# Four graph layers in fp32 on one core: the second half of the values moved ahead of the transposes of the exponentials, the adds of x moved behind the sums of k, and two outputs of layer 2's group 2 moved ahead of group 3's mix

## The chip, the cores and the metric

The kernel runs on one core of a Trainium2 chip, in one launch. The metric is the device time of that core in microseconds (us), the median of the runs. All data and all arithmetic are fp32.

## What is computed

The input x holds 128 samples of 64 nodes with 256 features each, 8192 rows ("tokens") in all, and adj is a 64 x 64 matrix that all samples share. Four layers are applied one after the other, each to the normalized and rectified x, and each result is added to x:

```
h = maximum(layernorm(x), 0);  x = x + gnn_lstm(h, adj)       # layer 0
h = maximum(layernorm(x), 0);  x = x + attention(h, W, adj)   # layer 1
h = maximum(layernorm(x), 0);  x = x + gcn(h, adj)            # layer 2
h = maximum(layernorm(x), 0);  x = x + three_slconvs(h, adj)  # layer 3
```

The change is in layers 1 and 2:

```
def attention(h, W, adj):                       # W is 256 x 768, 4 heads of 64
    q, k, v = split(h @ W)                      # per sample and head: 64 x 64 each
    scores = q k^T / 8 + where(adj == 0, -inf, 0)
    return softmax(scores) v                    # 64 x 64 scores per sample and head

def gcn(features, A):                           # W1 256 -> 512, W2 512 -> 256
    agg = A_hat @ features                      # A_hat: normalized A + I, 64 x 64
    h = relu(batchnorm(agg @ W1^T + b1))        # statistics over all 8192 tokens
    return batchnorm(h @ W2^T + b2)
```

Layer 0 is two graph convolutions and LSTMs over windows of one to four nodes. Layer 3 is three products of the form adj * (h W), 256 to 512 to 1024 to 256.

## The kernel before

**Tiles and order.** The 8192 tokens are worked on in 16 groups (`NG`) of 512 tokens (`GN`), that is 8 samples: four tiles of 128 partitions (two samples of 64 nodes) by 256 features. x stays in SBUF as 16 tiles `xs[g]`, and tiles are shared with other data before their x arrives. The code is written in program order; a scheduler in the framework orders the instructions of each engine and sets the semaphores, and `tc.issue_after(i)` keeps what stands inside it behind instruction i in that order. Each engine, and each DMA queue (SyncE's, SP, and GpSimd's, POOL), works through its own list in order. There are 8 PSUM banks of 128 x 512 fp32. One fp32 matmul shows as two records in the trace.

**The attention loop** runs over g = 0 to 15. What iteration g issues, in program order:

- `values(hT_all, v, (0,))`, the first half of the group's values: four matmuls (L1118, 8 records), one ScalarE copy of the bank to `vt` (L1123), and four DMAs on SP's queue (L1126) that put `vt` in order into `v`.
- for g = 4 to 7, `load_x` of x g+8 on SP.
- `queries_keys`: q and k by seven block products instead of eight. Products L1096; copies of two products to `p` on ScalarE (L256); two sums on VectorE (L262, L263). `finish()` adds the rest: the last sum of k on GpSimd (L267, put on the list `sums_on_pool`, whose last entry `summed_last()` gives), a quarter of q on ScalarE (L347), and two more sums on VectorE (L272, L278).
- `add_output(g - 2)`: o = attention output times the reciprocal sum, two VectorE operations (L1204), each followed by one on GpSimd that adds o to x (L1207). Then `sums_of()`, the sums of the exponentials of group g-1 and their reciprocals on VectorE (L1168, L1169).
- `turn(e)`: the exponentials of group g-1 are transposed on TensorE (L1179, 8 transposes, 16 records) into two banks, and each bank is copied by ScalarE to `eT` (L1182).
- `finish()` of the queries and keys.
- only in g = 15: the load of layer 2's first weights, `w1` (L1253), on SP's queue. It goes into the tile that held the weights of q and k, so it waits for the last product that reads them.
- `values(hT_all, v, (1,))`, the second half of the values, as the first. Behind its last DMA: `put_down()`, four DMAs on SP (L396) that write a transposed piece of layer 0's result to DRAM (for groups up to 8).
- `add_turned`: one accumulating DMA on GpSimd's queue (L404) that reads such a piece from DRAM and adds it to an x. It stands behind `shifts_made[g]`, the last GpSimd operation (L997) of the layernorm of group g.
- `features(transposed(h))` for group g+1: h transposed on TensorE (L128, 8 transposes), two ScalarE copies to `hT` (L415), and four differences of blocks of hT on VectorE (L419, L423, L424) for the seven products.
- `attend(eT, v_last)`: exponentials times values of group g-1 (L1192).
- `scores(q, k)`: L1143, and two VectorE operations that scale the scores and add the mask (L1150).
- `softmax`: maximum and subtraction on VectorE (L1161, L1162), the exponential on ScalarE (L1163).
- behind the subtraction: for g < 8 `turn_nodes` (L391, transposes on VectorE of layer 0's result), and `normalized(g + 2)`: the statistics of x (VectorE L991, L993, L994, L996), rstd and nmr on GpSimd (L995, L997), and four ScalarE operations that make h (L112). In g = 14 and 15 the h of layer 2's groups 0 and 1 is made in place of it, also in L112.

So the group whose values are made, the group whose scores are made and the group whose exponentials are turned overlap in one iteration.

**Around the end of the loop**, layer 2 starts: `mixed(g)` multiplies h by the normalized adjacency in 64 x 64 pieces (L146, 64 records) and two copies (L159) evict the two banks; `hidden_products(g, w1, ms)` makes the outputs ms, of four, of the first product (L1022, 4 records each, into one bank each); `hidden_out` takes the statistics of a bank on VectorE (L1033) and copies it to SBUF on ScalarE (L1034).

**Layer 2's loop** runs over g = 1 to 15. For g = 2 on, `mixed(g + 1)` goes ahead of the products of group g; `FREE_FIRST = (2, 3, 0, 1)` is the order of the four outputs. The groups in `SEVEN_FC1` (3, 4, 6, 7, 9, 10, 12) are made by seven block products (`hidden_seven`, L1055), for which `hidden_differences` makes differences of mixed blocks on GpSimd (L1041 to L1043). `rectified(g + 2)` makes h of a later group (L112), `scale(g + 3)` its statistics and scale.

Of the kernel before, what the change touches and what calls it, by code (L numbers as in the profile page):

```python
# [21 lines left out]
NG = NTOK // GN  # L22
# [3 lines left out]
NK = PER  # L26
# [13 lines left out]
def adj_preln_kernel(ctx: ExitStack, tc: tile.TileContext, x_in, adj, vec, bg0, bg1,  # L40
# [9 lines left out]
    def bank(shape=(P, 512)):  # L50
        return psp.tile(list(shape), F32, tag="ps", name="ps")
# [6 lines left out]
    def load_x(x, g):  # L58
        nc.sync.dma_start(out=x, in_=x_view[:, g * GT : (g + 1) * GT, :])
# [63 lines left out]
    def transposed(src):  # L123

        pss = [bank() for _ in range(2)]
        for c in range(2):
            for t in range(GT):
                nc.tensor.transpose(  # L128
                    pss[c][:, t * P : (t + 1) * P], src[:, t, c * P : (c + 1) * P], ident
                )  # L130
        return pss
# [37 lines left out]
    def summed_last():  # L169
        return sums_on_pool[-1]  # L170
# [229 lines left out]
    def add_turned(g):  # L400

        b0 = (g % PER) * GB
        y = ys[g // PER][b0 : b0 + GB].rearrange("(t b) n d -> (b n) t d", b=2)
        nc.gpsimd.dma_start(out=xs[g], in_=y, accum_op=ALU.add)  # L404
# [574 lines left out]
    FREE_FIRST = (2, 3, 0, 1)  # L979
# [33 lines left out]
    def hidden(g, w1, ms=range(4)):  # L1013
        return hidden_out(g, ms, hidden_products(g, w1, ms))

    def hidden_products(g, w1, ms):
        a = h1s[g]
        pss = []
        for m in ms:
            ps = bank()  # L1020
            for c in range(2):
                nc.tensor.matmul(  # L1022
                    ps, lhsT=w1[:, c, m * P : (m + 1) * P], rhs=a[:, 2 + c, :],
                    start=(c == 0), stop=(c == 1),
                )
            pss.append(ps)
        return pss
# [49 lines left out]
    with tc.tile_pool(name="att", bufs=2, reuse_waits="tile") as ap_:  # L1077
        shifts_made, outputs_added = [], []

        def normalized(g):  # L1080
            h = ap_.tile([P, GT, D], F32, tag="h", name="h")
            rstd, nmr, made = ln_on_pool(xs[g])
            ln_apply(xs[g], h, rstd, nmr)
            shifts_made.append(made)
            return h
# [24 lines left out]
        def values(hT, v, ks):  # L1110


            for k in ks:
                ps = bank((P, 2, D))
                for t in range(2):
                    tok = (2 * k + t) * P
                    for c in range(2):
                        nc.tensor.matmul(  # L1118
                            ps[:, t, :], lhsT=hT[:, c, tok : tok + P], rhs=wv[:, c, :],
                            start=(c == 0), stop=(c == 1),  # L1120
                        )
                vt = ap_.tile([P, 2, D], F32, tag="vt", name="vt")
                nc.scalar.copy(vt, ps)  # L1123
                for par in range(2):
                    for b in range(2):
                        last = nc.sync.dma_start(  # L1126
                            out=v[par * 64 : par * 64 + 64, 4 * k + b : 4 * k + 4 : 2, :],
                            in_=vt[b * 64 : b * 64 + 64, :, par * P : (par + 1) * P],
                        )
            return last.ins  # L1130
# [91 lines left out]
        for g in range(NG):  # L1222
            if g == NG - NK + 1:
                turn_pool.__exit__(None, None, None)
                hres_pool.__exit__(None, None, None)
                with tc.using_default_side("right"):
                    ar_right = ctx.enter_context(
                        tc.tile_pool(name="arena_r", bufs=NG // 2, reuse_waits="tile")
                    )
            hT_all, blocks = hT  # L1230
            v = ap_.tile([P, 2 * GT, P], F32, tag="v", name="v")
            moved = values(hT_all, v, (0,))
            if 0 <= g - NK < NK:
                with tc.issue_after(moved):
                    load_x(xs[g + 2 * NK], g + 2 * NK)
            q, k, finish = queries_keys(blocks)
            if g == 0:
                h = normalized(1)
            if last is not None:
                with tc.issue_after(finish.behind):  # L1240
                    if g > 1:
                        add_output(g - 2, pss, ri)
                    sums_of()
            if last is not None:
                e, ri, v_last = last
                if g > 1:
                    eT, turned = turn(e)
            added = finish()
            if g == NG - 1:

                w1 = w_att[:, :, 0:512]
                w2 = w_att[:, :, 512:1024].rearrange("p a (b f) -> a p b f", f=D)
                nc.sync.dma_start(out=w1, in_=w1t.rearrange("(c p) f -> p c f", p=P))  # L1253
            moved = values(hT_all, v, (1,))
            if put_down:
                with tc.issue_after(moved):
                    put_down()
            put_down = None
            if g == 1:

                eT, turned = turn(e)
            if 0 < g <= NG - NK:
                with tc.issue_after(shifts_made[g]):
                    if g > 4:
                        add_turned(g + NK - 1)
            if g + 1 < NG:
                hT = features(transposed(h))
            if g == 0:

                with tc.issue_after(last_copy.ins):  # L1270
                    nc.scalar.activation(rsum, mhalf[:, 0:1], AF.Exp)
            if g == NG - 1:
                turned_in = mixed(0, (on_scalar, on_scalar))
            if last is not None:
                pss = attend(eT, v_last)
            e_next = []

            def masked_scores():
                e, masked = scores(q, k)
                e_next.append(e)  # L1280
                return masked

            if g < NG - 1:
                masked_scores()
            else:
                with tc.issue_after(turned_in), tc.issue_after(added):
                    activated(ar_right, 1, masked_scores)
            ri_next, sub, sums_of = softmax(e_next[0])
            last = (e_next[0], ri_next, v)
            with tc.issue_after(sub):  # L1290
                if g < 8:
                    put_down = turn_nodes(
                        g + 8, tp.tile([P, TN, 2, 32], F32, tag="turned", name="turned")
                    )
                if g + 2 < NG:
                    h = normalized(g + 2)
                elif g + 2 == NG:
                    activated(ar_right, 0)
# [15 lines left out]
        pss = attend(eT, v_last)  # L1314
# [65 lines left out]
    for g in range(1, NG):  # L1380
        if g == 1:
            mixed(2, (on_scalar, on_scalar))
            counted[1] += hidden(1, w1, range(2))
        else:
            if g + 1 < NG:
                seven_next = g + 1 in SEVEN_FC1
                mixed(g + 1, (on_scalar, on_scalar if seven_next else on_vector))
                if seven_next:
                    hidden_differences(g + 1, fc1_t(g + 1))
            if g == SEVEN_FC1[-1] + 1:  # L1390
                for a in range(2):
                    nc.sync.dma_start(
                        out=w2[a], in_=w2t.rearrange("(a b p) f -> a p b f", a=2, p=P)[a]
                    )
            if g in SEVEN_FC1:
                counted.append(
                    hidden_seven(
                        g, fc1_w, fc1_t(g), lambda: rectified(g + 2), lambda last: scale(g + 3, last)
                    )
                )  # L1400
                continue
            pss = hidden_products(g, w1, FREE_FIRST)
            counted.append(hidden_out(g, FREE_FIRST[:1], pss))
            with tc.issue_after(evicted[-1]):
                last = rectified(g + 2)
            with tc.issue_after(last) if last else nullcontext():
                counted[g] += hidden_out(g, FREE_FIRST[1:], pss[1:])
        scale(g + 3, counted[g][2 if g == 1 else 0].ins)
        if g == 1:
            with tc.issue_after(evicted[-2]):  # L1410
                rectified(3)
# [92 lines left out]
    for g in range(NG):  # L1504
# [20 lines left out]
        else:  # L1525
            pss = first_pss[g] if g < 2 else [bank() for _ in range(2)]
# [369 lines left out]
    for g in range(NG + 1):  # L1896
# [13 lines left out]
        if s3 is not None:  # L1910
            pss = [bank((P, 2, D)) for _ in range(2)]
            if g == NG:
                pss = [pss, [bank((P, 2, D)) for _ in range(2)]]
# [92 lines left out]
```

## Time and profile before

| | us |
|---|---|
| three runs | 2420.54, 2420.59, 2421.62 |
| median | 2420.59 |
| the profiled execution, its own time | 2423.3 |
| its span in the trace | 2421.5 |

The busy time of each engine in stretches of the trace. The attention loop takes the third stretch, layer 2's first products are in the fourth.

| stretch, us | TensorE | VectorE | ScalarE | GpSimd | granted clock | DMA share |
|---|---|---|---|---|---|---|
| 0 to 600 (layer 0) | 595.30 | 463.77 | 350.23 | 172.43 | 1.00 | 0.08 |
| 600 to 1190 (layer 0) | 589.26 | 393.92 | 270.04 | 110.68 | 1.00 | 0.13 |
| 1190 to 1417 (layer 1) | 222.13 | 195.46 | 126.28 | 84.27 | 1.00 | 0.47 |
| 1417 to 1700 (layer 2) | 279.08 | 200.52 | 166.62 | 95.16 | 0.99 | 0.07 |
| 1700 to 2421 (layer 3) | 712.91 | 431.77 | 264.08 | 143.39 | 1.00 | 0.12 |

Times in the trace count from the start of the span. A line of the timeline gives the start, the duration, the engine, the line of the kernel, the operation, what is written and read, the shapes, the count of records that were merged, and in brackets how long the engine was idle before it and which engine and line ended that idle time. PE is a matmul on TensorE, PEld the load of its stationary operand, DVE is VectorE, ACT is ScalarE, POOL is GpSimd, SP is SyncE, and "q" behind an engine's name is its own queue of issues. A line of a table by stretches gives the stretch, its length, the busy time (and number of records) of PE, PEld, DVE, ACT and POOL, the granted TensorE clock (1.00 is full speed), the DMA share and GB/s.

### The profile page before, as it was taken

The numbers are of one execution on the slowest core, as the hardware profiler recorded it, in microseconds if no ns is written. First come the engines' busy times: TensorE is split into PE (matmuls) and PEld (weight loads), VectorE is DVE, ScalarE is ACT, GpSimd is POOL, SyncE is SP. The second block draws the span as 40 slices with busy tenths as digits, with TensorE's granted clock in tenths as the row PEclk, the third lists the DMA queues.
The fourth block names the chain that finished last, engine by engine and source line by source line (L and its number), as shares of the span: only waits on it lengthen the run. The fifth ranks groups of instructions, "written<-read, shape, count | busy, mean of one in ns | idle before, by whom it ended". The sixth has DMA issues, their size and how long they took to land.

```text
span 2421.5 us, 49124 instructions
## 1 busy us (share of the span) xinstructions
PE 2398.7 (99%) x20272; PEld 2094.3 (86%) x20272; DVE 1685.4 (70%) x3425; ACT 1177.2 (49%) x2178; POOL 605.9 (25%) x549
## 2 busy tenths in 40 slices
PE   9999999999999999999999999999999999999999
PEld 7778888889999999988888867586898999999998
DVE  6768888777566687775599887586556655665664
ACT  4557755555444454453455556564333334333332
POOL 4432222222111112212224444123111311221121
PEclk9999999999999999999999999999999999999999
DMA  4200000001000000053347410010133100000000
GB/s 139 86 2 1 1 18 1 1 1 35 1 1 1 1 1 1 18 127 70 53 78 133 76 32 2 10 62 10 27 62 57 33 10 11 19 10 10 19 10 19
DMA packets 163712, 75.45 MB, mean 31 GB/s; under 512 B 104481, under 2 KB 159905, under 8 KB 163489
## 3 DMA queue, kind: packets, MB, share of 16 engines
q1 hardware_dynamic: 150096, 59.18, 9.8%
q0 software_dynamic: 12672, 12.58, 3.5%
q8 instruction: 159, 2.61, 0.4%
q14 instruction: 65, 0.52, 0.1%
q10 hardware_dynamic: 720, 0.56, 0.1%
HBM read 42.94 MB, written 20.97 MB: 26 GB/s over the span
## 4 chain that ended last, share of the span: by engine, by line
PE 92%; DVE 5%; ACT 2%; issue 1%; POOL 0%; DVEq 0%; ACTq 0%; POOLq 0%
PE ps L704 37%; PE ps L1772 13%; PE ps L1824 8%; PE ps L197 7%; PE ps L1700 4%; PE ps L146 4%; PE ps L1096 3%; PE ps L612 2%; PE ps L638 2%; PE ps L1470 2%; PE ps L1022 2%; PE ps L1055 2%; PE ps L1532 1%; PE ps L1118 1%; PE ps L1845 1%
## 5 line engine op out<-in xcount | busy, mean ns | idle before, releaser
L718 ACT ACTIVATE gates<-gates,lbias 128x512 f32<-128x512 f32 (+3 forms) x482 | 265.7, 605 | 173.7 <-DVE gates L272 121.6
L704 PE MATMUL ps<-diff,s 128*128 128x256 f32 (+1 forms) x1600 | 344.9, 369 | 0.5 <-DVE diff L826 0.5
L704 PEld LDWEIGHTS ps<-diff,s 128*128 128x128 f32 x1600 | 303.3, 190 | 27.5 <-issue 0.9
L1772 PE MATMUL ps<-arena 128*128 128x256 f32 x1408 | 318.5, 380 | 0.0
L267 POOL TENSOR_TENSOR gates<-p 128x512 f32<-128x512 f32 (+1 forms) x115 | 148.9, 1295 | 589.0 <-DVE p L263 518.4
L1772 PEld LDWEIGHTS ps<-arena 128*128 128x128 f32 x1408 | 261.4, 190 | 35.1 <-issue 2.0
L704 PE MATMUL ps<-h,w 128*128 128x256 f32 (+1 forms) x1028 | 242.5, 371 | 0.0
L704 PE MATMUL ps<-diff,w 128*128 128x256 f32 (+1 forms) x1040 | 239.7, 371 | 0.0
L704 PEld LDWEIGHTS ps<-diff,w 128*128 128x128 f32 x1040 | 194.8, 190 | 16.5
L704 PEld LDWEIGHTS ps<-h,w 128*128 128x128 f32 x1028 | 192.7, 190 | 17.7 <-issue 0.5
L267 POOL TENSOR_TENSOR arena<-arena 128x512 f32<-128x512 f32 (+1 forms) x80 | 91.7, 1147 | 461.9 <-DVE arena L263 407.8
L256 ACT COPY p<-ps 128x512 f32<-128x512 f32 (+1 forms) x262 | 142.1, 563 | 60.1 <-PE ps L704 39.7
L350 ACT ACTIVATE arena<-arena 128x512 f32<-128x512 f32 x168 | 98.5, 624 | 121.4 <-POOL arena L267 66.5
L256 ACT COPY arena<-ps 128x512 f32<-128x512 f32 (+1 forms) x160 | 82.2, 517 | 149.6 <-PE ps L1700 59.5
L1824 PE MATMUL ps<-arena 128*128 128x128 f32 x1280 | 149.1, 275 | 0.8 <-DVE arena L339 0.8
L1824 PEld LDWEIGHTS ps<-arena 128*128 128x128 f32 x1280 | 146.7, 192 | 2.1 <-DVE arena L339 1.2
L718 ACT ACTIVATE gates<-ps,lbias 128x256 f32<-128x256 f32 (+2 forms) x157 | 68.2, 479 | 143.9 <-PE ps L704 143.8
L339 DVE TENSOR_TENSOR arena<-arena 128x512 f32<-128x512 f32 (+1 forms) x192 | 111.3, 612 | 29.4 <-ACT arena L350 27.8
L207 ACT COPY free<-ps 128x128 f32<-128x128 f32 x104 | 27.6, 265 | 208.0 <-PE ps L197 208.0
L272 DVE TENSOR_TENSOR gates<-p,ps 128x512 f32<-128x512 f32 (+1 forms) x115 | 76.3, 664 | 65.0 <-PE ps L704 64.2
L704 PE MATMUL ps<-state,s 128*128 128x256 f32 (+1 forms) x512 | 116.3, 370 | 0.6 <-ACT p L256 0.6
L272 DVE TENSOR_TENSOR arena<-arena,ps 128x512 f32<-128x512 f32 (+1 forms) x80 | 48.1, 601 | 87.0 <-PE ps L1824 50.4
(270 smaller groups left out, 4831.0 us busy)
## 6 DMA issues: line engine op xcount, KB each, us to landing
x<-in_x SPq DMA_DIRECT2D x23, 512.0 KB, 4.0
y<-turned SPq DMA_DIRECT2D x64, 128.0 KB, 3.3
v<-vt SPq DMA_DIRECT2D x128, 64.0 KB, 2.6
w<-in_wih SPq DMA_DIRECT2D x4, 1024.0 KB, 7.2
x_for_h<-in_x SPq DMA_DIRECT2D x8, 512.0 KB, 6.9
x<-y POOLq DMA_DIRECT2D x8, 512.0 KB, 6.3
x_for_h<-y POOLq DMA_DIRECT2D x8, 512.0 KB, 6.7
z<-w SPq DMA_DIRECT2D x64, 64.0 KB, 2.0
```

What stands on the lines that cost most here:

```text
L146: last = nc.tensor.matmul(pss[b][half * 64 : half * 64 + 64, c, t, :], lhsT=src[rows, t, col : col + 64], rhs=a2[rows, :], start=True, sto ...
L197: nc.tensor.matmul(q[k], lhsT=w, rhs=b, start=first and k == 0, stop=True, skip_group_check=True)
L256: copied = nc.scalar.copy(p1 if i == 1 else p5, ps[i])
L267: nc.gpsimd.tensor_tensor(out=out[1][1], in0=p1, in1=p5, op=ALU.add).ins
L272: nc.vector.tensor_tensor(out[0][1], p1, ps[5], ALU.add)
L339: last = eng.tensor_tensor(out=s, in0=p, in1=q, op=op)
L350: nc.scalar.activation(o, o, func)
L704: nc.tensor.matmul(ps[:, r], lhsT=wc[:, j, :], rhs=bc, start=first and r == 0 and c == 0, stop=True, skip_group_check=True,)
L718: nc.scalar.activation(o, ps, func, bias=lbias[:, col : col + 1])
L1700: nc.tensor.matmul(ps[:, t, :], lhsT=w[:, t * P : (t + 1) * P], rhs=b, start=first and t == 0, stop=True, skip_group_check=True,)
L1772: nc.tensor.matmul(ps[:, r, :], lhsT=w[:, c, col : col + P], rhs=b[:, c, :], start=first and r == 0 and c == 0, stop=c == 1, skip_group_ch ...
L1824: nc.tensor.matmul(ps[:, t, :], lhsT=w[:, c, t * P : (t + 1) * P], rhs=b[:, c, :], start=first and t == 0 and c == 0, stop=c == 3, skip_gr ...
```

## The change

Three edits of order; no operation is added or removed, apart from the number of the group to which an add of x belongs.

1. In the attention loop `values(hT_all, v, (1,))` now stands ahead of `turn(e)`, of `finish()` and, in g = 15, of the load of `w1`. It stood behind these three.
2. `add_turned` stands behind `summed_last()`, the last sum of k on GpSimd, where it stood behind the layernorm of group g. It runs for g = 4 to 11 and takes x g+4, where it ran for g = 5 to 12 and took x g+3. Both make the adds for x 8 to 15, the changed kernel one iteration earlier.
3. In layer 2's loop, g = 2: the outputs 2 and 3 of group 2 (`FREE_FIRST[:2]`) are issued ahead of `mixed(3)`, and the outputs 0 and 1 behind it. All four were behind it.

```diff
@@ attention loop, g = 0 to 15
                     sums_of()
+            moved = values(hT_all, v, (1,))
             if last is not None:
                 e, ri, v_last = last
                 if g > 1:
                     eT, turned = turn(e)
             added = finish()
             if g == NG - 1:
                 w1 = w_att[:, :, 0:512]
                 w2 = w_att[:, :, 512:1024].rearrange("p a (b f) -> a p b f", f=D)
                 nc.sync.dma_start(out=w1, in_=w1t.rearrange("(c p) f -> p c f", p=P))
-            moved = values(hT_all, v, (1,))
             if put_down:
                 with tc.issue_after(moved):
                     put_down()
@@
-            if 0 < g <= NG - NK:
-                with tc.issue_after(shifts_made[g]):
-                    if g > 4:
-                        add_turned(g + NK - 1)
+            if NK <= g < NG - NK:
+                with tc.issue_after(summed_last()):
+                    add_turned(g + NK)
@@ layer 2, g = 2 to 15
+            pss = hidden_products(g, w1, FREE_FIRST[:2]) if g == 2 else []
             if g + 1 < NG:
                 seven_next = g + 1 in SEVEN_FC1
                 mixed(g + 1, (on_scalar, on_scalar if seven_next else on_vector))
@@
-            pss = hidden_products(g, w1, FREE_FIRST)
+            pss += hidden_products(g, w1, FREE_FIRST[len(pss) :])
```

`NK` is 4, so `NG - NK` is 12.

## The prediction

> **What bounds the kernel now.** I read the page first, then the timeline of the attention groups engine by engine, then the timeline and the granted clock at the start of layer 2.
>
> ```profile
> span 2421.5 us, 49124 instructions
> PE 2398.7 (99%) x20272; PEld 2094.3 (86%) x20272; DVE 1685.4 (70%) x3425; ACT 1177.2 (49%) x2178; POOL 605.9 (25%) x549
> PE 92%; DVE 5%; ACT 2%; issue 1%; POOL 0%; DVEq 0%; ACTq 0%; POOLq 0%
> ```
>
> By the page TensorE is the bound. Stage by stage that is not so. One attention group (group 3), from one maximum L1161 to the next:
>
> ```profile
> 1239.81 1.22 DVE L1161 TENSOR_REDUCE mx<-e 128x16 f32<-128x1024 f32 x1
> ...
> 1243.57 0.86 PEld L1179 LDWEIGHTS ps<-ident,e 128*128 128x128 f32 x8 [0.31 <-ACT e L1163]
> ...
> 1247.20 2.08 ACT L112 ACTIVATE h<-x_for_h,nmr,rstd 128x256 f32<-128x256 f32 x4 [0.97 <-POOL nmr L997]
> ...
> 1249.18 0.57 ACT L1123 COPY vt<-ps 128x512 f32<-128x512 f32 x1
> ...
> 1249.69 1.08 ACT L415 COPY hT<-ps 128x512 f32<-128x512 f32 x2
> ...
> 1250.80 0.69 DVE L419 TENSOR_TENSOR hT<-hT 128x512 f32<-128x512 f32 x1 [0.79 <-ACT hT L415]
> ...
> 1252.33 1.28 DVE L1150 SCALAR_TENSOR_TENSOR e<-ps,mask 128x512 f32<-128x512 f32 x2
> ...
> 1253.65 1.22 DVE L1161 TENSOR_REDUCE mx<-e 128x16 f32<-128x1024 f32 x1
> ```
>
> The reader is to see a closed loop of 13.84 us: VectorE works without a gap from L1161 to the statistics, GpSimd makes nmr, ScalarE starts h 7.39 after L1161, hT's copies start 2.49 after h, L419 1.11 after them, L1150 1.53 after L419, the next L1161 1.32 later. Each waits for the one before. TensorE's own work in a group is less: group 14 ran in 13.59, start to start, with hardly a wait. So ScalarE's place in this loop is worth time, and TensorE's small waits are not.
>
> In groups 6 to 8 the loop is 15.10, 15.39 and 15.08, since GpSimd's k meets L419:
>
> ```profile
> 1291.97 1.72 POOL L267 TENSOR_TENSOR k<-p 128x512 f32<-128x512 f32 x1
> 1292.32 1.93 DVE L419 TENSOR_TENSOR hT<-hT 128x512 f32<-128x512 f32 x1 [0.81 <-ACT hT L415]
> ```
>
> L419, else 0.69, ends 0.56 after GpSimd does (1293.69, 1294.25).
>
> **The change, part by part.**
>
> *Values ahead of the transposes.* TensorE does the same matmuls: eight records of L1118 (1.73 us) now run in front of L1179. They cover the waits for the exponentials (0.31 above in the loader, 0.07 to 0.54 in the matmuls). I cost this at nothing, because the loop does not pass through L1179; were the loop gone, it would be worth the sum over groups 9 to 14, some 1.7, and about 1.3 in groups 2 to 8. But the built program's order moves ScalarE too. In groups 2 to 8 between h and hT stood one copy (vt, L1123); now stand the second eT copy (L1182) and q (L347), because vt goes ahead of h. One operation more, at the step of such copies, 0.48 (in group 9: 1335.08, 1335.54, 1336.02, 1336.51). So each of groups 2 to 5 takes 0.48 more: +1.92. In groups 9 to 14 the order becomes h, vt, eT, eT, q, hT: four operations. The trace has that count in group 9:
>
> ```profile
> 1333.10 2.08 ACT L112 ACTIVATE h<-x_for_h,nmr,rstd 128x256 f32<-128x256 f32 x4 [1.32 <-POOL nmr L997]
> ...
> 1336.97 1.09 ACT L415 COPY hT<-ps 128x512 f32<-128x512 f32 x2
> ```
>
> 3.87 from h to hT, and a loop of 14.06 (without the transposes L391 h starts 6.21 after L1161: 6.21 + 3.87 + 1.13 + 1.52 + 1.32). Groups 9 to 14 took 14.06, 13.80, 13.91, 14.01, 13.55 and 13.60; at 14.06 each the change is 0, +0.26, +0.15, +0.05, +0.51, +0.46: +1.43. Groups 0 and 1 keep their path.
>
> *Adds of x behind the sums of k.* By the built order GpSimd does k first, then the add's issue (L404), then the two L1207; the adds also start a group earlier, so group 8 has none. In groups 6 and 7 k is no longer late, but L1207 takes its place: k ends 1.19 after h starts, L404 takes 1.3, two L1207 2.54: GpSimd is busy until 5.03 after h, L419 is ready at 2.97 + 1.11 = 4.08 and would end at 4.77, and so ends at 5.59. The loop is 14.32 + 0.82 = 15.14, against 15.10 and 15.39: +0.04 and -0.25. Group 8 is 14.32 against 15.08: -0.76. No row shows L1207 holding up L419 for long; I price it by k's row, as the same operation on the same shapes. Bounds: no hold (-0.82 for each of two groups, -1.6), or a hold by the whole 1.24 of the row above (+0.8). Sum of both parts over groups 2 to 14: 1.92 + 1.43 + 0.04 - 0.25 - 0.76 = +2.4.
> [...]
>
> *The load of layer 2's weights.* This is what the diff hides. In group 15 values now stands ahead of the load of w1 (L1253) in the program and on SP's queue, where a transfer that waits holds up those behind it.
>
> ```profile
> 1417.18 0.40 SPq L1253 DMA_DIRECT2D w<-in_w1t  x1
> 1419.45 0.57 ACT L1123 COPY vt<-ps 128x512 f32<-128x512 f32 x1
> 1420.05 3.37 SPq L1126 DMA_DIRECT2D v<-vt  x4
> 1421.82 3.70 PE L1022 MATMUL ps<-arena,w 128*128 128x512 f32 x8
> ```
>
> Now w1 is issued as soon as the last product has read the old weights, 1417.18, and its landing takes 3.4 (the row of this transfer): 1420.6, 1.2 ahead of L1022. After the change it stands behind four v transfers that wait for vt, and ScalarE does vt right after the four L112 (h starts 7.18 after L1161, here too). vt ends 2.55 after h, four issues take 2.5 to 3.4 (such rows: 2.54, 2.61, 2.93, 3.37), the landing 3.4: w1 is there some 9.2 after h. L1022 started 4.83 after h (1416.99): +4.4. No other TensorE work stands in between, since its queue is in order. Bounds: 2.5 for the issues and the 2.6 that a v transfer takes to land, +3.3; 3.4 and the 5.1 of a 1024 KB load, +6.1. Without this reordering the cost is 0, and I see no gain in it. The old slack of 1.2 is used up within these figures.
>
> *Two outputs of group 2 ahead of group 3's mix.* There TensorE waits for L112 and then runs slow:
>
> ```profile
> 1441.58 1.44 PE L146 MATMUL ps<-ah,arena 64*64 64x64 f32 x48 [1.37 <-ACT arena L112]
> 1443.50:1444.50 1.00, 1.00 (x6) 0.07 (x5) 0.40 (x1) 0.00 (x0) 0.92 (x2) 0.51 0.00 0
> ```
>
> The granted clock is 0.5 from 1443.5 to about 1446.9: 3.4 us at half speed, 1.7 lost. Before: from the end of group 1's outputs (1440.06) to the end of group 3's products (1459.52) 19.4. After, by rows: wait for L159 0.2, eight records of L1022 3.55, mix L146 1.05, eight records 3.55, mix 1.05. ScalarE now does group 4's L112 (ready at 1446.0 by nmr, 2.08) and an eviction before it copies group 3's mix: the copies end about 1449.6, GpSimd's L1041 at 1450.9. So a wait of 0.2, one product 0.86, a wait of 0.55, six products 5.3. Together 16.3: -3.1. With no wait at all it would be -3.9; if the late copies cost twice as much, -2.3.
>
> *Clock after the new stall.* TensorE idles some 4.3 us before L1022. No row shows so long a wait; the nearest is the 1.37 above, followed by 3.4 us at half clock: +1.7. Bounds: 0, and two such stretches less the idle part, +2.7. I take +1.7.
> [...]
>
> **Sum:** +2.4 + 4.4 + 1.7 - 3.1 = +5.4. The profiled execution took 2423.3 (span 2421.5 and 1.8 around it), 2.7 over the median of the runs, 2420.59; the difference is put on the median: 2426.0, +0.22%. With each term at its end: -1.6 - 1.1 - 1.7 - 0.8 below and +0.8 + 1.7 + 1.0 + 0.8 above; not all at once, so the forecast's own range is 2422.5 to 2429.5.
>
> **Rivals.**
> 1. *w1 comes in time* (SP's transfers pass each other, or vt is done earlier). For it: only one load; against it: the built order and the 1.2 of slack. The terms 4.4 and 1.7 fall away: 2419.9.
> 2. *ScalarE's order costs nothing and the loop opens.* TensorE then sets the pace in attention: the covered exponentials (3.0) and k's three waits of 0.58 (1.7) come off, and w1 is hidden; with layer 2's 3.1: 2412.8, faster. For it: TensorE is 99% busy and the waits named at L1179 and L1143 are the ones edited. Against it: periods of 13.84, 13.83 and 13.83 with VectorE idle for one wait of 0.79. It decides if h comes no later and hT's copies follow it by 2.49 or less.
> 3. *The clock falls in attention too.* The loop leaves TensorE idle 0.5 to 1.5 per group, split up; in group 15 about 1.3 around L146. Half clock twice more: +3.4, 2429.4. Against it: groups 6 to 8 had such idle time at full clock.
>
> **How the numbers follow.** Forecast 0.57, rival 1 0.15, rival 2 0.13, rival 3 0.15. The likeliest gives 2426.0. The range runs from 2418.5 (below rival 1) to 2430.5 (above rival 3) and leaves out rival 2 and a little above: 2 in 10. A difference of 0.2% (4.8 us) is about what a measurement can tell from none: over 2425.4 lie a good half of the forecast and rival 3, 0.48; under 2415.8 rival 2, 0.12; the rest, 0.40, between.
>
> **What would show it.** Groups 2 to 5 at 14.3 from L1161 to L1161, with L1182 and L347 between L112 and L415; groups 9 to 14 at 14.06; no wait left at L1179; L419 stretched in groups 6 and 7 by L1207 and not in 8; w1's load behind four v loads and L1022 waiting some 4 us for it; half clock after that and none at group 3's mix. I am wrong if those groups run at 13.6, or if L1022 follows the scores at once.

## The result, and the profile after

The changed kernel took 2431.47 us (median of 6 runs, 2428.85 to 2432.59) against 2421.56 for the kernel before on the same chip (6 runs, 2420.54 to 2424.14): a ratio of 1.0038, interval 1.0026 to 1.0051. It is slower by about 9.9 us. The forecast had the side right and the amount too small: 2426.0, and 2431.47 lies above the end of its range, 2430.5.

The first lines of the page of the changed kernel, its busy times and the shares of the chain that ended last:

```profile
span 2430.8 us, 49154 instructions
PE 2399.5 (99%) x20272; PEld 2099.4 (86%) x20272; DVE 1681.9 (69%) x3425; ACT 1174.7 (48%) x2178; POOL 606.2 (25%) x549
PE 91%; DVE 5%; ACT 2%; issue 1%; POOL 1%; DMA 1%; SPq 0%; DVEq 0%; ACTq 0%; POOLq 0%
```

The work is the same (20272 records on TensorE in both), and TensorE's busy time has hardly moved (2398.7 before). Of the 9.3 us between the two spans 0.8 are busy time of TensorE; the rest is waiting. New in the chain is a DMA, 1%. The page can't say more, since a share is a mean over all stages.

Group 3 of the attention loop in the timeline of the changed kernel (start, duration, engine, line; all engines, the lines of the loop picked out):

```profile
1242.25 1.22 DVE L1161 TENSOR_REDUCE mx<-e 128x16 f32<-128x1024 f32 x1
...
1249.63 2.08 ACT L112 ACTIVATE h<-x_for_h,nmr,rstd 128x256 f32<-128x256 f32 x4 [1.08 <-POOL nmr L997]
...
1251.62 0.56 ACT L1182 COPY eT<-ps 128x512 f32<-128x512 f32 x1
...
1252.09 0.58 ACT L347 ACTIVATE q<-ps 128x512 f32<-128x512 f32 x1
...
1252.57 1.05 ACT L415 COPY hT<-ps 128x512 f32<-128x512 f32 x2
...
1253.65 0.69 DVE L419 TENSOR_TENSOR hT<-hT 128x512 f32<-128x512 f32 x1 [1.21 <-ACT hT L415]
...
1256.50 1.22 DVE L1161 TENSOR_REDUCE mx<-e 128x16 f32<-128x1024 f32 x1
```

Two ScalarE operations, eT and q, now stand between h and hT, where vt alone stood before. hT starts 2.94 after h (2.49 before), L419 waits 1.21 for it (0.79 before), and the group takes 14.25 (13.84 before).

The end of the loop, TensorE alone, then the granted clock in stretches (start and end, length, busy time and records of PE, PEld, DVE, ACT, POOL, then the clock, 0.50 in the second row):

```profile
1425.03 1.14 PE L1143 MATMUL ps<-k,q 64*64 64x64 f32 x63
1430.64 5.37 PE L1022 MATMUL ps<-arena,w 128*128 128x512 f32 x8 [4.48 <-DMA w<-in_w1t]
1435.94 1.16 PE L146 MATMUL ps<-ah,arena 64*64 64x64 f32 x64
```

```profile
1430.00:1431.00 1.00, 0.36 (x1) 0.30 (x2) 0.16 (x1) 0.81 (x1) 0.00 (x0) 1.00 0.01 2
1431.10:1434.50 3.40, 3.40 (x5) 1.35 (x4) 0.52 (x1) 0.15 (x1) 0.00 (x0) 0.50 0.00 0
1435.00:1439.00 4.00, 4.00 (x72) 2.22 (x71) 2.95 (x12) 1.91 (x4) 0.02 (x1) 1.00 0.01 4
```

TensorE waits 4.48 for w1, and then runs 3.4 us at half clock: eight records of L1022 take 5.37, where they took 3.70.

All profiles of this case side by side, cut at the same instructions. "Values" is the first L1118, the next columns run from there to the first L1022, from that to the first L1055, to the first L1700 (layer 3), to the end of the last matmul, and to the end of the span. The last column counts TensorE's waits for its own instructions ("issue") in front of L146 in layer 3, and their sum. The kernels other than the two are those of the experiments below.

| kernel | start to values | to L1022 | to L1055 | to L1700 | layer 3 | rest | waits at L146 |
|---|---|---|---|---|---|---|---|
| before | 1197.27 | 224.55 | 31.46 | 211.67 | 752.53 | 4.03 | 4, 3.7 |
| before_again | 1199.35 | 224.59 | 29.89 | 211.67 | 752.57 | 4.01 | 4, 3.5 |
| after | 1199.29 | 231.35 | 29.23 | 211.66 | 753.94 | 5.34 | 6, 4.9 |
| after_again | 1199.03 | 231.53 | 29.19 | 211.66 | 754.73 | 4.01 | 6, 5.3 |
| w1_first | 1199.29 | 226.46 | 27.91 | 211.98 | 755.66 | 4.71 | 7, 6.1 |
| l2_only | 1197.25 | 224.63 | 27.90 | 211.98 | 752.22 | 4.01 | 4, 3.0 |
| values_only | 1196.48 | 227.71 | 31.46 | 211.67 | 755.29 | 5.92 | 7, 5.6 |
| adds_only | 1197.29 | 223.91 | 29.89 | 211.68 | 753.13 | 4.01 | 4, 4.1 |
| adds_last | 1196.21 | 220.73 | 27.90 | 211.97 | 752.57 | 4.02 | 4, 3.5 |
| values_middle | 1197.25 | 224.07 | 27.82 | 211.97 | 754.03 | 4.01 | 4, 4.0 |
| pad64 | 1201.22 | 225.39 | 29.89 | 211.66 | 756.62 | 4.01 | 7, 7.2 |

So between the two first profiles 2.0 come before the change begins, 6.8 from attention with the load of w1, -2.2 from layer 2, +1.4 from layer 3, and +1.3 from the last landing. Only the second and third belong to lines that the change touches. Whether the others belong to it was the first question.

### The profile page after: what moved, and what is told of

It is laid out like the page before. It is cut to its first block, busy times and chain, and to the rows that moved or that the text cites. A ratio compares the mean times of both kernels' runs of the same rounds, so it can differ in the third digit from the quotient of the medians.

```text
span 2430.8 us, 49154 instructions
## 1 busy us (share of the span) xinstructions
PE 2399.5 (99%) x20272; PEld 2099.4 (86%) x20272; DVE 1681.9 (69%) x3425; ACT 1174.7 (48%) x2178; POOL 606.2 (25%) x549
## 4 chain that ended last, share of the span: by engine, by line
PE 91%; DVE 5%; ACT 2%; issue 1%; POOL 1%; DMA 1%; SPq 0%; DVEq 0%; ACTq 0%; POOLq 0%
PE ps L704 37%; PE ps L1772 13%; PE ps L1824 8%; PE ps L197 7%; PE ps L1700 4%; PE ps L146 4%; PE ps L1022 3%; PE ps L612 3%; PE ps L638 2%; PE ps L1470 2%; PE ps L1055 2%; PE ps L1096 2%; PE ps L1532 1%; PE ps L1118 1%; ACT h L112 1%
## 5 line engine op out<-in xcount | busy, mean ns | idle before, releaser
L1772 PE MATMUL ps<-arena 128*128 128x256 f32 x1408 | 318.4, 381 | 0.0
L1772 PEld LDWEIGHTS ps<-arena 128*128 128x128 f32 x1408 | 262.0, 191 | 34.4 <-issue 1.7
```

The costliest lines, as they stand in the source:

```text
L1772: nc.tensor.matmul(ps[:, r, :], lhsT=w[:, c, col : col + P], rhs=b[:, c, :], start=first and r == 0 and c == 0, stop=c == 1, skip_group_ch ...
```

## The experiments

### The kernel before and the changed kernel once more

> The kernel before, unchanged. Theory (some of the difference is not of the change): the stretch up to the first values, 1197.3 us in the first profile, and the landing of the last output differ from run to run by up to 2 us, while layer 3 has the same four waits of TensorE for its own instructions at the same matmuls as before (0.86, 1.09, 1.19, 0.60, sum 3.7), since they come from the place of the instructions in the program. Rival (these waits are chance as well): other waits, at other matmuls. Time 2420.5 to 2424.

> The changed kernel, unchanged. Theory: from the first values to layer 3 it takes 4.6 more than the kernel before (472.3 against 467.7), and layer 3 has the same six waits for instructions as in its first profile (sum 4.9, 1.1 more than before): 2421.6 + 5.7 = 2427.3, and what is above that is the start-up (1199.3 instead of 1197.3 up to the first values) and the last landing, by chance. Rival (the start-up is slower by the change): again 1199 or more up to the first values, 2431.

before_again: 2423.92 us against 2421.93 for the runs beside it, ratio 1.0003 (0.9994 to 1.0012). after_again: 2430.71, ratio 1.0034 (1.0021 to 1.0046).

The stretch up to the values was 1197.27 and 1199.35 for the same kernel: that difference is chance (what it goes with is in the last section). Layer 3 repeats: four waits at L146 in both profiles of the kernel before, at the same instructions, six in both of the changed one. So the 1.4 to 2.2 of layer 3 belong to the change, though no line of layer 3 is in it. The forecast of 2427.3 for the changed kernel was too low again.

before_again had a surprise in layer 2. TensorE alone, at group 3's mix, and the granted clock behind it:

```profile
1443.71 1.44 PE L146 MATMUL ps<-ah,arena 64*64 64x64 f32 x48 [1.38 <-ACT arena L112]
1445.08 1.13 PE L1022 MATMUL ps<-arena,w 128*128 128x512 f32 x2
1446.14 0.46 PE L146 MATMUL ps<-ah,arena 64*64 64x64 f32 x16
1446.53 6.28 PE L1022 MATMUL ps<-arena,w 128*128 128x512 f32 x14
```

```profile
1445.50:1448.90 3.40, 3.40 (x24) 1.50 (x23) 1.73 (x4) 1.60 (x4) 3.11 (x5) 1.00 0.02 5
```

The same wait, 1.38, but the clock stays at 1.00, and the stretch to L1055 takes 29.89, not 31.46. Of the five profiles without the edit in layer 2, two fell to half clock here (31.46) and three did not (29.89). More executions agree: of 73 of the kernel before, 23 have a mean granted clock of 0.998 or 0.999 and 50 of 1.000 (one stretch of 3.4 us at half clock takes 0.0007 off the mean). So at most about a third of them fell here.

### The load of w1

In the changed kernel, group 15 alone makes the second half of its values behind the load:

```diff
-            moved = values(hT_all, v, (1,))
+            if g < NG - 1:
+                moved = values(hT_all, v, (1,))
...
                 nc.sync.dma_start(out=w1, in_=w1t.rearrange("(c p) f -> p c f", p=P))
+                moved = values(hT_all, v, (1,))
```

> The changed kernel, but group 15 makes the second half of its values behind the load of layer 2's weights, as before the change. Theory: the load is issued when the last product has read the old weights, the 4.45 of waiting in front of L1022 and the half clock behind it (1.67) go, from the first values to L1022 it takes 224.55 + 2.1 = 226.7 (231.35 in the changed kernel), and the time falls by 6.1 to 6.5, to some 2425. Rival (another wait takes the place of the load, such as the copies of eT or the scores): 229 or more to L1022, and 2429 or more.

2425.23 us, ratio to the kernel before 1.0014 (1.0005 to 1.0022), so 5.5 to 6.2 less than the changed kernel. SP's queue and L1022 in the timeline of the changed kernel, and then of w1_first:

```profile
1413.77 12.96 SPq L1126 DMA_DIRECT2D v<-vt  x8
...
1422.88 0.56 ACT L1123 COPY vt<-ps 128x512 f32<-128x512 f32 x1
...
1426.83 0.54 SPq L1254 DMA_DIRECT2D w<-in_w1t  x1
```

```profile
1421.07 0.40 SPq L1255 DMA_DIRECT2D w<-in_w1t  x1
1423.96 3.48 SPq L1126 DMA_DIRECT2D v<-vt  x4
...
1425.74 3.70 PE L1022 MATMUL ps<-arena,w 128*128 128x512 f32 x8
```

In the changed kernel the load stands behind eight v transfers, of which the last four wait for the vt of 1422.88; it is issued at 1426.83 and L1022 starts 3.8 later. In w1_first it is issued at 1421.07 and waits for nobody's vt: L1022 comes with no wait, at full clock (3.70). From the values to L1022 it takes 226.46 (expected 226.7). By the stretches of the table this is the largest single cost of the change: 231.35 against 226.46 up to L1022, and 29.23 against 27.91 behind it.

### Layer 2's edit alone

```diff
+            pss = hidden_products(g, w1, FREE_FIRST[:2]) if g == 2 else []
...
-            pss = hidden_products(g, w1, FREE_FIRST)
+            pss += hidden_products(g, w1, FREE_FIRST[len(pss) :])
```

> The kernel before with the edit in layer 2 alone. Theory: no wait for L112 and no half clock at group 3's mix; from the first L1022 to the first L1055 27.6 instead of 31.5 (less 1.37 of waiting, 1.7 of clock and the rest of the mix in pieces), 2421.6 - 3.9 = 2417.7; layer 3's waits for instructions as before (one instruction of TensorE more). Rival (only the wait goes, the clock falls elsewhere): 29.3 and 2419.4. Rival (the late copies of group 3's mix take it back): 31 and 2421.

2419.55 us, ratio 0.9991 (0.9982 to 1.0001): a gain of 2.4, at the edge of what can be told. To L1055 it took 27.90, near the 27.6 of the theory; but the theory counted from 31.46, and 29.89 is as common. Layer 2 after it is 0.3 longer (211.98). So the edit brings 1.7 where the clock would have held and 3.25 where not. Four kernels have this edit and get w1 in time. In three of them (l2_only, and adds_last and values_middle below) the mean granted clock is 1.000 in all 31 runs; w1_first has 3 of 11 below that, and in the profiled one of these the half clock is at the start.

### Values alone, adds alone

values_only is the kernel before with this alone, so that group 15 keeps its order:

```diff
                     sums_of()
+            if g < NG - 1:
+                moved = values(hT_all, v, (1,))
...
                 nc.sync.dma_start(out=w1, in_=w1t.rearrange("(c p) f -> p c f", p=P))
-            moved = values(hT_all, v, (1,))
+                moved = values(hT_all, v, (1,))
```

adds_only is the kernel before with this alone:

```diff
-            if 0 < g <= NG - NK:
-                with tc.issue_after(shifts_made[g]):
-                    if g > 4:
-                        add_turned(g + NK - 1)
+            if NK <= g < NG - NK:
+                with tc.issue_after(summed_last()):
+                    add_turned(g + NK)
```

> The kernel before with the values moved alone, and group 15's behind the load of w1. Theory (ScalarE's place in the loop): groups 2 to 5 at 14.25 and 9 to 14 at 14.05 from one maximum to the next, as in the changed kernel; 6 to 8 15.1 to 15.5, since k still meets L419; from the first values to L1022 224.6 + 3.1 = 227.7 or a little more. TensorE has 33 instructions more, so layer 3 has six or more waits for instructions at its mixes (before: four). Rival (the adds make the groups longer, not ScalarE): 13.83 in groups 2 to 5 and 224.6 or less.

> The kernel before with the adds of x moved alone. Theory: groups 2 to 5 at 13.83; in groups 6 and 7 k comes in time and L1207 holds L419 by 0.8, 14.7; group 8 13.84; one of groups 9 to 11, where one L1207 stands between L995 and L997 on GpSimd, up to 1.2 longer; from the first values to L1022 222.7 to 224 (224.6 before). [...] Rival (the adds make the loop longer): 14.2 in groups 2 to 5. TensorE's instructions are as many as before: four waits in layer 3's mixes.

From one maximum to the next (the difference of the starts of L1161), in us:

| groups | before | after | values_only | adds_only | adds_last | values_middle |
|---|---|---|---|---|---|---|
| 2 | 13.77 | 14.19 | 14.19 | 13.78 | 13.76 | 14.19 |
| 3, 4, 5 (mean) | 13.83 | 14.25 | 14.26 | 13.84 | 13.83 | 14.26 |
| 6 | 15.10 | 15.10 | 15.10 | 15.10 | 13.85 | 14.27 |
| 7 | 15.39 | 15.08 | 15.39 | 15.10 | 13.87 | 14.29 |
| 8 | 15.08 | 14.26 | 15.10 | 13.85 | 13.86 | 14.28 |
| 9 to 14 (mean) | 13.82 | 14.05 | 14.06 | 13.97 | 13.85 | 13.91 |

values_only: 2430.30 us, ratio 1.0031 (1.0019 to 1.0043), and 227.71 to L1022, as expected. The values alone, with w1 in time, are the slower loop. Of the 7.6 us between the medians that is 3.2; in the profile layer 3 is 2.7 longer and the last landing 1.9 longer than in the kernel before. adds_only: 2421.19, ratio 0.9997 (0.9988 to 1.0006). Group 8 came as expected, 6 and 7 not: 15.10, not 14.7. The timeline of group 6 in adds_only says why:

```profile
1288.69 1.26 POOL L267 TENSOR_TENSOR k<-p 128x512 f32<-128x512 f32 x1
...
1289.91 1.30 POOL L404 DMA_DIRECT2D x_for_h<-y  x1
...
1290.75 3.00 POOL L1207 TENSOR_TENSOR x_for_h<-x_for_h,o 128x512 f32<-128x512 f32 x2
1292.37 1.94 DVE L419 TENSOR_TENSOR hT<-hT 128x512 f32<-128x512 f32 x1 [0.81 <-ACT hT L415]
```

L419 starts 0.4 earlier behind h than in the changed kernel (3.60 against 4.03) but does not end before L1207: it ends at 1294.31, 0.56 after GpSimd (1293.75), the same 0.56 as behind k in the kernel before. The group's end is set by when GpSimd is done, so the hold simply takes up what L419 was earlier.

### The adds behind GpSimd's other work

If so, the add's issue (L404, 1.3) must not stand ahead of L1207. adds_last is the kernel before with the edit in layer 2 and

```diff
+            if NK <= g < NG - NK:
+                with tc.issue_after(summed_last()), tc.issue_after(outputs_added[-1]):
+                    add_turned(g + NK)
```

in place of the add of the kernel before. One more line differs, in adds_last and in values_middle: the sums of blocks of layer 2's weights on GpSimd (`sums(nc.gpsimd, *fc1_a[0], *fc1_a[1], *fc1_s)`) stand behind `summed_last()` too, and not behind `outputs_added[-1]` alone. No run has that line by itself; behind L1022 adds_last and l2_only take the same time up to layer 3 (27.90 and 211.97 or 211.98).

> The kernel before with the edit in layer 2, and the adds of x behind the sums of k and behind both L1207 of the group as well; values and load of w1 as before. Theory: with GpSimd's order k, L1207, L1207, L404 neither k nor L1207 meets L419; groups 6 to 8 at 13.84 instead of 15.10, 15.39 and 15.08 (less 4.0), one of groups 9 to 11 up to 1.2 longer; with layer 2's 2.0, 2421.9 - 4.8 to - 6.0 = 2416 to 2417. Rival (L1207 still holds L419): 14.7 in groups 6 and 7, 2418.

2416.15 us, ratio to the kernel before 0.9977 (0.9967 to 0.9986): faster than both, by the adds and the edit in layer 2 together. Group 6 in its timeline:

```profile
1287.57 1.27 POOL L267 TENSOR_TENSOR k<-p 128x512 f32<-128x512 f32 x1
...
1288.80 2.53 POOL L1207 TENSOR_TENSOR x_for_h<-x_for_h,o 128x512 f32<-128x512 f32 x2
1291.24 1.30 POOL L404 DMA_DIRECT2D x_for_h<-y  x1
1291.24 0.69 DVE L419 TENSOR_TENSOR hT<-hT 128x512 f32<-128x512 f32 x1 [0.80 <-ACT hT L415]
```

Now L1207 is done as L419 starts, and L419 takes 0.69. The issue L404 beside it holds nothing up. Groups 6 to 8 are at 13.85 to 13.87, and attention to L1022 is 220.73, 3.8 less than before.

### TensorE's order or ScalarE's?

values_only moves two things: TensorE makes the values ahead of the transposes, and ScalarE's copies change places. values_middle is adds_last with this:

```diff
                     eT, turned = turn(e)
+            if g < NG - 1:
+                moved = values(hT_all, v, (1,))
             added = finish()
...
                 nc.sync.dma_start(out=w1, in_=w1t.rearrange("(c p) f -> p c f", p=P))
-            moved = values(hT_all, v, (1,))
+                moved = values(hT_all, v, (1,))
```

TensorE's transposes then go ahead of these values, as before; but between h and hT ScalarE does vt and q.

> The kernel adds_last with the second half of the values between the transposes of the exponentials and the rest of the products (group 15 as before, behind the load of w1). TensorE then makes the transposes ahead of these values, as in the kernel before; on ScalarE vt and q stand between h and hT, two operations, as eT and q do in the changed kernel (one in the kernel before). Theory (the count of copies between h and hT sets the group): groups 2 to 5 at 14.25, 6 to 8 at 14.25 or a little more, from the first values to L1022 2.5 to 4 longer than in adds_last (220.73). Rival (TensorE's order, values ahead of transposes, made the groups longer): 13.84 and 220.7.

2419.36 us, ratio 0.9987 (0.9977 to 0.9996), a smaller gain than that of adds_last. Groups 2 to 8 at 14.19 to 14.29, and to L1022 224.07, 3.3 more than in adds_last. ScalarE in group 3:

```profile
1247.59 2.08 ACT L112 ACTIVATE h<-x_for_h,nmr,rstd 128x256 f32<-128x256 f32 x4 [1.99 <-POOL nmr L997]
1249.58 0.57 ACT L1123 COPY vt<-ps 128x512 f32<-128x512 f32 x1
1250.04 0.59 ACT L347 ACTIVATE q<-ps 128x512 f32<-128x512 f32 x1
1250.53 1.06 ACT L415 COPY hT<-ps 128x512 f32<-128x512 f32 x2
```

Two operations between h and hT, vt and q where the changed kernel has eT and q, and the same 2.94 from h to hT; the groups take 14.26. Values ahead of the transposes are not the cause, since here they stand behind them. ScalarE's rows have no gap from h to hT, and L419 waits for hT: the count of operations there is what makes the group longer.

### Sixteen small products at the start

Why does layer 3 change? Its waits of TensorE are for "issue", for nothing that another engine does. Counting TensorE's records in the trace in order of their start, from 0 (weight loads, matmuls and waits on semaphores), the waits of 0.6 and more in front of L146 stand at numbers 30657, 31681, 35521 and 36545 before, and 28865, 30657, 31681, 32705, 36545 and 37569 after: all 193 more than a multiple of 256. The page of the kernel before lists among the DMA queues (queue, kind: packets, MB, share of 16 engines):

```profile
q8 instruction: 159, 2.61, 0.4%
```

Each packet of it in the trace has 16384 bytes (16 KB), and the trace has 160 of them, the last one behind the span. TensorE's program has 40897 records there, which in pieces of 256 are 160 as well. From these two counts, a packet for each 256 instructions of TensorE is an estimate of the author's. The waits go with the packets: in all eleven profiles each of the 57 waits in front of L146 ended 1.2 to 1.6 us after a packet of this queue did. So they are taken here as waits for instructions. The changed order gives TensorE 36 instructions more (386 waits on semaphores in place of 350), so everything behind stands elsewhere in its pieces of 256. To test this, the kernel before was given 64 instructions more:

```diff
             keep_busy(7)
+            for i in range(16):
+                half = slice(i % 2 * 64, i % 2 * 64 + 64)
+                nc.tensor.matmul(
+                    idle[half, 0:1], lhsT=ones[half, 0:64], rhs=ones[half, 0:1],
+                    start=True, stop=True,
+                )
```

> The kernel before with 16 small products (64 x 64 by one column, 64 instructions of TensorE) more at the start, while TensorE waits for adj; nothing of them is used. Theory (layer 3's waits come where the 16 KB pieces of TensorE's instructions end inside a mix): all instructions behind move by 64 places, and layer 3's mixes have eight or nine waits instead of four, at other matmuls, layer 3 takes 756 to 758 instead of 752.5, though nothing of it was changed. Rival (chance, or transfers at the same time): the same four waits at the same matmuls, 752.5.

2429.59 us, ratio 1.0028 (1.0016 to 1.0040). Some 3 of it are the start (the products delay the first values to 1201.22) and 0.8 is attention; layer 3 took 756.62, as expected, with seven waits at L146 (eight or nine were expected). One spot, TensorE in the kernel before and then in pad64, which is here 4.5 us later:

```profile
1913.43 0.61 PE L1845 MATMUL ps<-arena,w2s 64*64 64x256 f32 x8
1913.86 0.51 PE L146 MATMUL ps<-w2s,arena 64*64 64x64 f32 x20
1915.23 0.92 PE L146 MATMUL ps<-w2s,arena 64*64 64x64 f32 x44 [0.86 <-issue]
```

```profile
1917.96 0.61 PE L1851 MATMUL ps<-arena,w2s 64*64 64x256 f32 x8
1918.40 1.11 PE L146 MATMUL ps<-w2s,arena 64*64 64x64 f32 x64
1919.44 5.45 PE L1778 MATMUL ps<-arena 128*128 128x256 f32 x24
```

The wait there is gone, and others have come, at 1825.72, 2013.61 and 2061.39 among them, where the kernel before has none. In all eleven profiles such waits stand 193 or 194 past a multiple of 256, and where one kernel was profiled twice they are at the same matmuls. So in these runs the waits go by the place of the instructions, and each ends 1.2 to 1.6 us after a packet; why one packet comes later than another is open.

## Why the prediction was wrong, point by point

- **What bounds attention** held: the loop through VectorE, GpSimd and ScalarE. TensorE's waits at L1179 did not vanish as forecast: 0.29 to 0.43 is left in groups 2 to 6, and 1.1 in 7 and 8; by the profile they end with L262, not with the exponentials. It cost nothing, as the loop does not pass there.
- **Values ahead of the transposes**: forecast 0.48 in each of groups 2 to 5 and +1.43 over 9 to 14; measured 0.42 each and +1.35. values_middle agrees with the reason given, the count of ScalarE's operations between h and hT.
- **Adds of x**: forecast +0.04, -0.25 and -0.76 in groups 6 to 8; measured 0.00, -0.31 and -0.82. The price taken from k's row for L1207 was right: L419 took 0.69 with GpSimd done and 1.51 to 1.94 beside L1207. Why GpSimd's operation holds it up is not shown.
- **w1**: forecast +4.4, measured 4.8 (from L1022 1.83 ahead of the last L1161 to 2.96 behind it). w1_first showed the cause.
- **Clock after the stall**: forecast +1.7; L1022's first eight records took 1.67 more, and of that 1.0 was left by layer 3 (240.89 from L1022 to L1700, 239.88 in l2_only).
- **Layer 2's edit**: here a step failed in size. "The granted clock is 0.5 from 1443.5 to about 1446.9: 3.4 us at half speed, 1.7 lost" took one execution's clock for a property of the kernel. Without the half clock the stretch was 29.89, and the edit is worth 2.0 there and 1.7 to layer 3, not the 3.1 of the sum; with it, 3.25. The profiled execution stood 2.7 over the median of the runs, which was a sign that the median need not have that half clock, and 50 of 73 executions have a mean clock of 1.000. The range had bounds for the edit's waits, and none for this.
- **Layer 3**: here a step failed by being left out. Layer 3 stood in the sum at nothing, without a reason, and was not a rival. The change puts 36 instructions into TensorE's program ahead of it, and layer 3 takes 754.34 instead of 752.55 in the mean of two profiles each, +1.8, by waits for instructions. pad64 showed that moving the instructions alone does this.
- **The base**: 2420.59 was the median of three runs; in later comparisons the kernel before took 2421.56 to 2423.45.

By the means of two profiles each, the difference is +0.9 at the start, +6.9 in attention, -1.5 to L1055, +1.8 in layer 3 and +0.7 at the end: 8.7, against 9.9 and 8.8 by the medians. In the stretches that the sum was about, attention and layer 2, this makes +5.4, just the forecast. In layer 2 that is partly luck: one of the two profiles of the kernel before had the half clock, and the smaller gain of the edit and the smaller loss behind the stall (1.0 and not 1.7) hide each other. What the sum lacked is layer 3, and the 1.5 of the start and the last landing. Whether the change has a part in those two stays open. The last landing was 4.0 in eight of the profiles, and 4.71, 5.34 and 5.92 in three. At the start the kernel before shows both 1197.27 and 1199.35; but 6 of the 11 executions of the changed kernel have a mean granted clock of 0.998 or less, of the kernel before 1 of 73, and the 3.4 us at half clock behind L1022 take only 0.0007 off the changed kernel's.

## What to carry to other kernels

Ask of every move of code what it does to the order on the engines that it doesn't name: here one copy more on ScalarE between h and hT (0.42 a group in groups 2 to 5) and one load behind four waiting transfers on SP's queue (4.48 of waiting in front of L1022) cost more than the waits that the move covered. Count the issue of a DMA too: in adds_only L404 took 1.30 on GpSimd ahead of L1207, and L419 ended 0.56 after GpSimd did. Put last, it held nothing up (adds_last, groups 6 to 8 at 13.85 to 13.87 where they took 15.08 to 15.39). And before a gain is counted from a stretch at half clock, look at a second profile.

## What the runs showed of the hardware

- **Waits for instructions came with their place.** Where 256 instructions of TensorE pass in some 2.2 us (64 x 64 products), it waited 0.6 to 1.4 us at some of the places 193 or 194 past a multiple of 256. A change far ahead moved these places: layer 3 took 752.2 to 753.1 us in the kernels with 350 or 351 waits on semaphores in TensorE's program, 754.0 with 356 (values_middle, which has two more waits at such places, 0.18 and 0.76 in front of L1772 right behind a mix), 753.9 to 755.7 with 383 to 386, and 756.6 with the 64 instructions of pad64. None of these kernels is without such waits.
- **The start-up went with the clock.** The records of the granted clock show when it became full for good: after 5.4, 6.0, 9.6, 9.7, 9.8, 9.9, 14.0, 14.1, 14.3 and 14.6 us, and the first values came at 1196.48, 1196.21, 1197.29, 1197.25, 1197.25, 1197.27, 1199.03, 1199.35, 1199.29 and 1199.29 in the same order, with the same lines up to there. That is a spread of 3 us before the change begins; one kernel alone, the kernel before, shows 2.1 of it.
- **Half clock came in whole pieces** inside the span: 3.41 us, and 6.83 at the start of two profiles. In every profile the changes of the clock inside the span lie whole multiples of 3.413 us apart (420 and 285 of them in the kernel before). Why the same wait of 1.38 brought a half clock in two profiles and none in three is not shown. In the two, the 3.41 us ahead of the half clock held the whole wait and the narrow products of L146, and other matmuls filled 0.19 of it; in the three, with the trace cut at the same multiples, other matmuls filled 0.25, 0.44 and 0.47 of the stretch that held most or all of the wait. Five profiles are too few to tell whether that decides. The 4.5 in front of L1022 brought the half clock in both profiles that had it, and all 11 executions of the changed kernel have a mean granted clock of 0.997 to 0.999.
